# Two PSUM tiles of the item part move to another pool, and the first two inputs to another DMA queue, in a GRU, attention and AUGRU kernel

## The chip, the cores and the metric

The kernel runs on one core of one Trainium2 chip. The metric is device time in microseconds (us). Four runs of the kernel before had a median of 2054.43 us, from 2053.69 to 2054.89.

## What is computed

A recommendation model with 1024 users (B), histories of 100 steps (T) and 128 features. The reference, cut down:

```python
keys = scan(gru_step, h0, x)                       # GRU over T steps
feat = concat([keys, q, keys - q, q * keys])       # q: the item, the same at every step
score = mlp(feat, att_W0..2)                       # 512 -> 80 -> 40 -> 1, relu
attn = softmax(where(mask == 1, score, -inf), over T)
pooled = einsum('bt,btd->bd', attn, keys)
att_seq = pooled.T[:T]
aug = scan(augru_step, h0, (keys, att_seq))        # a second GRU, its update gate weighted by att_seq
attention_feature = aug[sequential_length - 1]
scores = mlp(concat([user, item, hist_sum, item * hist_sum, attention_feature]), ph_W0..2)
```

Since q is the same at all steps, the first attention layer is split: a part of the keys and of q*keys at each step, and an item part, computed once (the kernel's `q0`).

## The kernel before, in words

The batch is split into two halves of 512 columns (HB). Features lie on the 128 partitions. The program has two phases, one after the other.

**GRU phase** (`gru_phase`). A loop over 100 steps s, and in each step over the halves. A step of a half (`Half.gru`) opens gate tiles of 128x512 in PSUM (helper `gate`, L499, matmuls at L501): `ps0` (reset), `ps2` twice (the hidden and the input share of the new state) and `ps1` (update), six matmuls of f32, each of which TensorE runs as two passes. ScalarE takes the sigmoid of the reset gate (L513); VectorE forms `u` (L521) and adds it to the input share (L531); ScalarE takes tanh (L532) and the update gate's sigmoid (L533), both in place; VectorE finishes with `d` (L536, L537) and the new state `hn` (L538). At step 0 there is no old state and only the input matmuls run.

After both halves of step s comes `attend(s - 1)` (L656, matmuls at L663), which writes two tiles `pm`, one a half, with all layers of the attention's MLP for earlier steps packed side by side. Two steps later `take` (L687) reads them: VectorE adds the item part `q0` (L697), ScalarE applies relu (L702). At step 1 alone, `item_part` (L236) runs between the gates and `attend(0)`: for each half a matmul of the item into a tile `pq` (L239), then a ScalarE activation that moves it to `q0` with a bias (L242).

PSUM has eight banks of 128x512 f32. The pool `ps` (tag "g", six buffers) holds the gate tiles, one tile `count`, and at the end of the phase six tiles named `last`; the pool `pa` (tag "a", two buffers) holds `pq`, `pm` and `pt`. A tile that takes a buffer waits until the tile that had it before has been read for the last time. In the compiled program a pool hands its buffers out in the order in which the program's build sees them released: the gate tiles of step 1 lie in banks 0, 3, 4, 5 (half 0: reset, hidden share, input share, update) and 0, 2, 1, 3 (half 1), those of step 2 in 0, 5, 4, 2 and 3, 1, 0, 5; `pq` lies in banks 6 and 7, as do all `pm`.

**Start.** SP's queue issues, in this order: the weights `wih` (L182), `x_first` (L185, step 0 of half 0), the biases `bih` and `bhh` (L124), `x_second` (L189, step 0 of half 1), `whh` (L124), the inputs of steps 1 and 2 (L471), and the attention's weights (L220 to L234). ScalarE's first instruction of the program is an activation on a one-column tile (L198) that brings the table load forward.

**End of the GRU phase.** L876 takes the six `ps` buffers as `last`: two for the softmax (`e`), one for its transposes (`pt`), one for VectorE's pooling products (`kw`), two for the features' matmuls (`f`). In the compiled program they lie in banks 1, 3, 0, 4, 2 and 5. VectorE and GpSimd finish the pooling (L589, L599, L600), VectorE writes it to `s_b` (L937), and eight DMAs store it in `pooled_d` (five on SP's queue, three on ScalarE's, L941 and L1208).

**AUGRU phase** (`augru_phase`). It has one pool for each of banks 0 to 6 and one for bank 7. It loads keys with transposes on TensorE (L1040) that ScalarE copies (L1041), computes first gates (L981), gathers the pooled rows by GpSimd (L144, `att_r`), and opens the first gate tiles (L1054) in banks that are fixed by number in L73: `FREE_BANK, EARLY_BANKS, LATE_BANKS = 6, (2, 5, 6, 0), (3, 4, 1)`; half 1's gates of step 1 in 2, 5, 6, a tile `spare` in 0, half 0's gates in 3, 4, 1. The attention's rows are spread by matmuls at L996 (`first`, `spare`), and then the loop over steps 1 to 99 follows.

Here stand the functions that the change touches:

Of the kernel before, what the change touches and what calls it, by code (L numbers as in the profile page):

```python
# [9 lines left out]
F32 = mybir.dt.float32  # L10
# [9 lines left out]
P = 128  # L20
B = 1024
T = 100
HB = 512
# [55 lines left out]
def kernel(ctx: ExitStack, tc: tile.TileContext, a: dict, out: bass.AP):  # L79
# [26 lines left out]
    nc = tc.nc  # L106
# [73 lines left out]
    def gru_phase(pools):  # L180
# [1 line left out]
        nc.sync.dma_start(out=wih, in_=a["wih"])  # L182
        xp = pools.enter_context(tc.tile_pool(name="xp", bufs=8))
        x_first = xp.tile([P, HB], F32, name="x")
        nc.sync.dma_start(out=x_first, in_=a["hist_x"][0][:, :HB])  # L185
        bih = load("bih", [P, 3])
        bhh = load("bhh", [P, 3])
        x_second = xp.tile([P, HB], F32, name="x")
        nc.sync.dma_start(out=x_second, in_=a["hist_x"][0][:, HB:])  # L189
        whh = load("whh", [P, 3, P])  # L190
        pre = pools.enter_context(tc.tile_pool(name="pre", bufs=1))

# [23 lines left out]
        ps = pools.enter_context(tc.tile_pool(name="ps", bufs=6, space=PSUM))  # L216
        pa = pools.enter_context(tc.tile_pool(name="pa", bufs=2, space=PSUM))
# [17 lines left out]

        def item_part():  # L236
            for i in range(NH):
                pq = pa.tile([P, HB], F32, tag="a", name="pq")
                nc.tensor.matmul(  # L239
                    pq, lhsT=wq[i], rhs=item[:, ts(i, HB)], start=True, stop=True  # L240
                )
                nc.scalar.activation(q0[:, ts(i, HB)], pq, AF.Identity, bias=bm[i])  # L242
# [211 lines left out]
        class Half:  # L454
# [13 lines left out]
            def load(self, t, again=False):  # L468
                if t or again:
                    x = xp.tile([P, HB], F32, name="x")  # L470
                    nc.sync.dma_start(out=x, in_=a["hist_x"][t][:, self.cols])  # L471
                    self.x[t] = x
# [339 lines left out]
        for s in range(T):  # L812
# [36 lines left out]
            if s == 0:  # L849
                attention_weights()  # L850
            else:
                if not staged:
                    next(rest, None)
                if s == 1:
                    item_part()
                attend(s - 1)
# [393 lines left out]
    with ExitStack() as pools, tc.manual_schedule():  # L1250
        gru_phase(pools)
# [79 lines left out]
```

## Time and profile before

| what | value |
|---|---|
| median of 4 runs (lowest to highest) | 2054.43 us (2053.69 to 2054.89) |
| the profiled execution's own time | 2052.77 us |
| span of its profile, first to last instruction | 2050.9 us |
| TensorE (PE) busy | 2022.3 us, 99% of the span |
| VectorE (DVE) busy | 1749.7 us, 85% |
| GpSimd (POOL) busy | 1303.4 us, 64% |
| ScalarE (ACT) busy | 830.6 us, 40% |
| DMA moved | 204.36 MB, mean 100 GB/s |

The page lists, for each engine, busy time and, for groups of instructions, how long the engine was idle just before them and what ended that. A timeline row reads: start in us from the span's start, duration, engine, line, operation, output<-inputs, shape, count of merged instructions, and in brackets the idle time before with its releaser. SPq and ACTq are DMA issues of SP's and ScalarE's queues. PEld is the weight load that precedes each pass of a matmul. Ends of matmuls are modelled and overlap the next one's start, so the distance between starts is the rate. Of the 2050.9 us the GRU phase takes about 1435 to 1447, the AUGRU phase the rest; the two engines that compute most, PE and DVE, are both busy across nearly all of it.

### The profile page before, as it was taken

To read this page: it belongs to the slowest core of one execution; us is meant where nothing else is said; L and a number is where in the kernel's file an instruction comes from. 1 tells how busy PE (TensorE), PEld (TensorE's weight loads), DVE (VectorE), ACT (ScalarE), POOL (GpSimd) and SP (SyncE) were. 2 spreads that over 40 slices of the span, in tenths; PEclk is the share of its full clock that TensorE was granted. 3 is DMA by queue.
4 is the path that set the end of the run, shared out by engine and by line. 5 is a ranking of instruction groups with operands and counts; after the bars stand their busy time and mean duration, and the time that the engine had idled before them with its cause. 6 is when DMAs were issued, how large, how long until landed. Compare 5 with 4: busy or idle time off the path is not lost. (4 is left out here: it accounts for less than half of the span.)

```text
span 2050.9 us, 26797 instructions
## 1 busy us (share of the span) xinstructions
PE 2022.3 (99%) x8320; PEld 978.1 (48%) x8320; DVE 1749.7 (85%) x3050; ACT 830.6 (40%) x1516; POOL 1303.4 (64%) x1299
## 2 busy tenths in 40 slices
PE   8999999999999999999999999999899999999998
PEld 3343343333333333333333333334444556678998
DVE  6888999998989988988889898999567777888886
ACT  3334343343433333433334333434344444445554
POOL 0233939669796959596896868898645434444432
PEclk9999999999999999999999999999999999999999
DMA  4643333223334334333333333332434333333332
GB/s 119 118 94 89 104 99 102 85 83 104 112 101 109 117 97 126 112 97 94 96 115 104 98 95 104 96 98 81 137 104 115 93 90 99 95 96 101 95 77 37
DMA packets 254132, 204.36 MB, mean 100 GB/s; under 512 B 76006, under 2 KB 217034, under 8 KB 253978
## 3 DMA queue, kind: packets, MB, share of 16 engines
q1 hardware_dynamic: 240266, 170.43, 29.4%
q0 software_dynamic: 12128, 31.91, 5.5%
q8 instruction: 68, 1.11, 0.2%
q14 instruction: 86, 0.70, 0.1%
q10 hardware_dynamic: 1584, 0.20, 0.1%
HBM read 146.43 MB, written 54.40 MB: 98 GB/s over the span
## 5 line engine op out<-in xcount | busy, mean ns | idle before, releaser
L501 PE MATMUL ps<-x,wih 128*128 128x512 f32 x1200 | 592.0, 603 | 4.1 <-DMA x<-in_hist_x 4.1
L501 PE MATMUL ps<-hn,whh 128*128 128x512 f32 x1188 | 574.4, 592 | 0.0
L501 PEld LDWEIGHTS ps<-x,wih 128*128 128x128 f32 x1200 | 220.6, 190 | 327.2 <-issue 254.6
L501 PEld LDWEIGHTS ps<-hn,whh 128*128 128x128 f32 x1188 | 225.7, 190 | 284.1 <-issue 274.1
L487 POOL TENSOR_TENSOR xm<-x,m 128x512 f32<-128x512 f32 x200 | 248.3, 1241 | 136.1 <-DMA m<-mask_d 135.6
L532 ACT ACTIVATE ps<-ps,bih 128x512 f32<-128x512 f32 x200 | 132.4, 662 | 478.7 <-DVE ps L531 478.7
L513 ACT ACTIVATE r<-ps,brz 128x512 f32<-128x512 f32 x200 | 137.5, 688 | 382.0 <-PE ps L501 381.1
L488 POOL TENSOR_TENSOR hist<-hist,xm 128x512 f32<-128x512 f32 x200 | 267.7, 1338 | 15.7
L600 POOL TENSOR_TENSOR pooled<-pooled,kw 128x512 f32<-128x512 f32 x191 | 254.0, 1330 | 15.0
L599 POOL TENSOR_TENSOR kw<-kt,e 128x512 f32<-128x512 f32 x191 | 219.5, 1149 | 64.7 <-DVE e L772 64.6
L168 POOL DMA_INDIRECT rows<-keys_d,idx_k x204 | 198.8, 975 | 81.6 <-POOL rows L167 75.5
L576 DVE TENSOR_TENSOR kq<-hn,item 128x512 f32<-128x512 f32 x200 | 224.5, 1162 | 0.0
L663 PE MATMUL pm<-hn,wk 128*32 128x512 f32 x1200 | 211.6, 596 | 3.8 <-ACT q L242 2.3
L663 PE MATMUL pm<-kq,wkq 128*32 128x512 f32 x1200 | 209.2, 592 | 0.0
L1066 ACT ACTIVATE c<-ph,bh 128x96 f32<-128x96 f32 (+41 forms) x198 | 96.5, 488 | 256.7 <-PE ph L1058 256.6
L663 PE MATMUL pm<-mv,w 128*32 128x512 f32 (+1 forms) x808 | 195.8, 598 | 1.3 <-DVE e L753 1.3
L697 DVE TENSOR_TENSOR f<-pm,q 128x512 f32<-128x512 f32 x200 | 128.3, 683 | 52.6 <-PE pm L663 52.6
L536 DVE TENSOR_TENSOR d<-hn,ps 128x512 f32<-128x512 f32 x198 | 136.0, 687 | 34.9 <-ACT ps L532 32.5
L167 POOL COPY rows<-rest 128x1 f32<-128x1 f32 x204 | 38.7, 190 | 199.0 <-DVE rest L1095 197.7
L1082 DVE TENSOR_TENSOR pu<-pu,c 128x96 f32<-128x96 f32 (+41 forms) x197 | 88.4, 449 | 88.5 <-ACT c L1066 84.6
L537 DVE TENSOR_TENSOR d<-ps,d 128x512 f32<-128x512 f32 x200 | 138.4, 692 | 23.6 <-ACT ps L533 6.5
L531 DVE TENSOR_TENSOR ps<-ps,u 128x512 f32<-128x512 f32 x200 | 140.0, 700 | 21.6 <-PE ps L501 0.5
(180 smaller groups left out, 3018.2 us busy)
## 6 DMA issues: line engine op xcount, KB each, us to landing
x<-in_hist_x SPq DMA_DIRECT2D x212, 256.0 KB
keys_d<-kt SPq DMA_DIRECT2D x46, 1024.0 KB
m<-mask_d SPq DMA_DIRECT2D x200, 128.0 KB
keys_d<-kt SPq DMA_DIRECT2D x64, 64.0 KB
rows<-keys_d,idx_k POOLq DMA_INDIRECT x204, 2.9
s_b<-mv SPq DMA_DIRECT2D x200, 8.0 KB
at<-att_d SPq DMA_DIRECT2D x34, 48.0 KB
mask_i<-in_mask SPq DMA_DIRECT2D x8, 200.0 KB
```

Source lines behind the costliest of these rows:

```text
L168: nc.gpsimd.indirect_dma_start(out=r[:, k, :], out_offset=None, in_=keys_d[q], in_offset=bass.IndirectOffsetOnAxis(ap=idx_k[:, k, i : i + ...
L487: nc.gpsimd.tensor_mul(d, x, m)
L488: nc.gpsimd.tensor_add(acc, acc, d)
L501: nc.tensor.matmul(p, lhsT=w[:, g, :], rhs=v, start=(j == 0), stop=(j == len(parts) - 1),)
L513: nc.scalar.activation(r, pr, AF.Sigmoid, bias=brz[:, 0:1])
L531: nc.vector.tensor_add(pi, pi, u)
L536: nc.vector.tensor_sub(d, h, pi)
L537: nc.vector.tensor_mul(d, pz, d)
L576: nc.vector.tensor_mul(kq, h, item[:, self.cols])
L599: eng.tensor_mul(d, k, w)
L600: eng.tensor_add(acc, acc, d)
L663: nc.tensor.matmul(p[i][s, :], lhsT=w[:, s], rhs=v, start=start, stop=stop)
```

## The change

The two first inputs are loaded through ScalarE's DMA queue instead of SP's, ahead of everything else on ScalarE. The two `pq` tiles come from the pool `ps` (tag "g") instead of `pa` (tag "a"). The whole diff:

```diff
@@ -182,11 +182,11 @@
         nc.sync.dma_start(out=wih, in_=a["wih"])
         xp = pools.enter_context(tc.tile_pool(name="xp", bufs=8))
         x_first = xp.tile([P, HB], F32, name="x")
-        nc.sync.dma_start(out=x_first, in_=a["hist_x"][0][:, :HB])
+        nc.scalar.dma_start(out=x_first, in_=a["hist_x"][0][:, :HB])
         bih = load("bih", [P, 3])
         bhh = load("bhh", [P, 3])
         x_second = xp.tile([P, HB], F32, name="x")
-        nc.sync.dma_start(out=x_second, in_=a["hist_x"][0][:, HB:])
+        nc.scalar.dma_start(out=x_second, in_=a["hist_x"][0][:, HB:])
         whh = load("whh", [P, 3, P])
         pre = pools.enter_context(tc.tile_pool(name="pre", bufs=1))
 
@@ -235,7 +235,7 @@
 
         def item_part():
             for i in range(NH):
-                pq = pa.tile([P, HB], F32, tag="a", name="pq")
+                pq = ps.tile([P, HB], F32, tag="g", name="pq")
                 nc.tensor.matmul(
                     pq, lhsT=wq[i], rhs=item[:, ts(i, HB)], start=True, stop=True
                 )
```

`FREE_BANK`, `EARLY_BANKS` and `LATE_BANKS` (L73) stay as they are.

## The prediction

> **What bounds the kernel now.** I read the page's first part (who is busy), then whom TensorE (PE) waits for, then the timeline of the stretches that the change touches.
>
> ```profile
> PE 2022.3 (99%) x8320; PEld 978.1 (48%) x8320; DVE 1749.7 (85%) x3050; ACT 830.6 (40%) x1516; POOL 1303.4 (64%) x1299
> ```
>
> PE works 99% of the span, so only time in which it stands or runs slowly can be won. The view of PE's waits from 0 to 1400 us is short (us in total, times, longest):
>
> ```profile
> PE ps L501 <- DMA x<-in_hist_x: 4.1, 1, 4.1
> PE pm L663 <- ACT q L242: 2.3, 1, 2.3
> PE pm L663 <- DVE e L753: 1.3, 1, 1.3
> ```
>
> The change touches the first (the first input) and the second (the item part). After the second PE runs at its own rate: step 2 starts at 30.06 and step 5 at 72.27 in the timeline, (72.27 - 30.06)/3 = 14.07 a step, and the step from 1384.89 to 1398.96 still takes 14.07. So what PE wins before 30 us should last to the end of the GRU phase. The timeline from there (rows of several engines):
>
> ```profile
> 20.79 0.69 ACT L513 ACTIVATE r<-ps,brz 128x512 f32<-128x512 f32 x1
> ...
> 21.12 0.69 DVE L537 TENSOR_TENSOR d<-ps,d 128x512 f32<-128x512 f32 x1
> ...
> 21.75 1.88 PE L239 MATMUL pq<-item,wq 128*128 128x512 f32 x4
> ...
> 21.84 0.69 DVE L538 TENSOR_TENSOR hn<-ps,d 128x512 f32<-128x512 f32 x1
> ...
> 24.62 0.65 ACT L533 ACTIVATE ps<-ps,brz 128x512 f32<-128x512 f32 x1
> ...
> 25.19 1.27 ACT L242 ACTIVATE q<-pq,bm 128x512 f32<-128x512 f32 x2
> ...
> 25.93 0.62 PE L663 MATMUL pm<-hn,wk 128*32 128x512 f32 x2 [2.30 <-ACT q L242]
> ...
> 26.51 0.11 PEld L663 LDWEIGHTS pm<-hist,w 128*32 128x32 f32 x1 [0.36 <-ACT q L242]
> ...
> 30.06 1.13 PE L501 MATMUL ps<-x,wih 128*128 128x512 f32 x2
> ```
>
> PE has the item part done by about 23.5, but `attend(0)` writes its `pm` into the two banks that `pq` fills, and ScalarE empties them only at 25.19, behind half 1's tanh and sigmoid of step 1. The second `pm` waits once more, in the middle of `attend(0)`.
>
> The start, in the timeline and in the DMA view of 0 to 6 us (GB/s in slices of 0.15 us):
>
> ```profile
> 0.74 1.28 ACT L198 ACT_TABLE_LOAD   x1 [0.74 <-PEq L1318]
> ...
> 0.75 0.39 SPq L182 DMA_DIRECT2D wih<-in_wih  x1
> 1.19 0.42 SPq L185 DMA_DIRECT2D x<-in_hist_x  x1
> ```
>
> ```profile
> GB/s 0 0 0 0 0 0 0 0 0 0 0 61 184 276 317 311 263 280 328 287 274 262 170 59 47 206 259 300 232 253 222 246 287 369 294 331 277 263 232 273
> ```
>
> The issues come 0.44 apart, and the DMA engines move some 260 to 330 GB/s from 1.95 on, with a hollow at 3.45 to 3.75. By the packet records, `wih` runs from 1.76 to 2.75 and `x_first` from 2.35 to 3.63. PE starts at 4.06, 0.43 after the last byte.
>
> **The item part.** Nothing is added: the same two matmuls and two activations, in other banks. Three steps.
>
> 1. Does `pq` still start at 21.75? It takes the two banks of `ps` that were released first. In the compiled order step 2 takes 0 and then 5 at this place: half 1's reset gate, read by ScalarE from 20.79 to 21.48, and half 0's update gate, read at L537 until 21.81. The first is free before 21.75, the second before 22.61, when `pq` of half 1 is due (two passes of 0.43 later). No wait. If the pool went by turn instead, `pq` would get half 0's input share, read until 22.53 (L538), and start 0.85 later. I take 0, with 0.85 as the other end.
> 2. The wait goes. Four passes at 0.43 end at 21.75 + 1.72 = 23.47. At step 4 `attend` follows its gates by 0.10 (67.74 + 0.86 = 68.60, against its start at 68.70), so `attend(0)` starts at 23.57, not 25.93: 2.36 less. What is next late? Its inputs: the state `hn` of step 0 (15.69), `kq` (16.85 + 1.28 = 18.13), the weights `w12`, whose last issue is at 18.43 now and earlier after, and which no row shows PE waiting for. None is later than 23.57.
> 3. The second wait goes. `attend(0)` takes 30.06 - 25.93 = 4.13, but 72.27 - 68.70 = 3.57 at step 4: in the timeline the streams that should run four abreast are out of step after 26.51. Another 0.56.
>
> Step 2 would then start at 23.57 + 3.57 = 27.14, that is 2.92 earlier. It needs half 0's `hn` (22.53) and a free bank: six have been released by 26.94 (half 1's L538). VectorE is done at 26.94 and then waited 3.30 us for `pm`, so its next row (L697) follows PE. `q0` is ready at 26.46 for it: the activations keep their place on ScalarE. The gain is 2.92, between 2.92 - 0.85 = 2.07 and 2.92 as far as these rows go.
>
> **The first inputs.** ScalarE issues two DMAs before its table load. I cost these two issues on ScalarE at nothing: 2 x 0.44 move the load from 0.74 to 1.63 and its end to 2.91, and ScalarE's next work is at 6.14; if that cover were gone it would be 0.9. On SP the rest moves up by 0.9, of which nothing is waited for. `x_first` is issued at 0.74 instead of 1.19, so 0.45 is the most it can win. But it then shares the engines with `wih`: 192 + 256 KB = 458,752 bytes at 280 GB/s are 1.64, from 1.75 to 3.39, plus 0.43, so PE starts near 3.8: 0.25 to 0.3. At the low end, ScalarE's table load stays ahead of the issues: `x_first` goes out at 2.07, 0.88 later than now, and PE loses 0.88. I take a gain of 0.3, since the first table load belongs to L198, behind the DMAs in the program; ends -0.88 and +0.45. [...]
>
> **Banks behind the GRU phase.** The names in L73 now point at other tiles of the phase's end. That costs something only if a first gate falls on a bank that is read late. The last read of any is VectorE's L600, which ends at 1446.88, and PE's wait view shows `pr` at L1054 waiting for just that (0.3 us) before the change too. Behind it are these rows:
>
> ```profile
> 1450.39 1.12 PE L1054 MATMUL pu<-k,wu 128*128 128x510 f32 x2 [1.49 <-ACT k L1041]
> ...
> 1459.63 1.22 PE L996 MATMUL first<-ident,att_r 128*128 128x128 f32 x4 [2.17 <-DMA att_r<-pooled_d,idx]
> ```
>
> PE is idle for 2.17 before the gathered rows arrive, and these come from VectorE by a DMA and GpSimd, not from a PSUM bank. That cover hides up to 2.17; I take 0.
>
> **The sum.** 2.92 + 0.3 = 3.2 us. The profiled execution's 2052.77 (span 2050.9 and 1.9 around it) would be 2049.6; the median of the runs is 1.7 above that execution, and I put the gain on it: 2054.43 - 3.2 = **2051.2 us**, 0.16% less. That is below the 0.2% (4.1 us, so 2050.3 and 2058.5) that a measurement of this kernel can tell from no change.
>
> **Rivals.**
>
> *More.* The starts of PE's weight loads are 0.86 apart up to 8.45 and 0.43 after, and from 1459 to 1463 the granted clock is 0.57: a drop behind the idle stretch. If the drop stays away when the program lies 3 us earlier, the four passes of `first` (1.22 there, 0.92 at 1456.55) and the eight of `spare` (1.91, later 1.05) are 1.2 shorter, about half of it on the path through L1007: 0.5 to 1.2 more, 2050.0 to 2050.7. For: the phases move against each other. Against: 2.17 of idle time stays. [...]
>
> *Less.* The table load comes first: 2.92 - 0.88 = 2.0 gained, 2052.4.
>
> *Nothing.* The end of the GRU phase follows VectorE, not PE (PE waits 1.54 for L697 at 1414.63), and VectorE, if it were late all along, would not move: 2054.4. Against: in the loop VectorE waits 50 times for `pm`.
>
> *Slower.* The pool gives `pq` a bank that half 1 still uses. The place is 21.75: with half 1's input share, read until 26.94 (L538), `pq` starts at 27.0, `attend(0)` runs from 28.82 to 32.39, 2.3 after 30.06; less 0.3, that is 2056.4, and 2057.6 with the late table load. It decides from a release at 30.06 - 3.57 - 0.10 - 1.72 - 0.06 = 24.6 on; only half 1's update gate (26.21) and input share are later. Against: the order of step 2 puts these two last.
>
> **How the numbers follow.** As forecast 0.58 (2051.2, by itself 2050.4 to 2052.0), more 0.14, less 0.13, nothing 0.08, slower 0.07. The range of 2050.0 to 2053.4 leaves out the last two and the far end of "more". Faster by over 0.2% is most of "more" and a little of the forecast's edge: 0.13. Slower by over 0.2% needs the slower rival and one more loss: 0.03. The rest, 0.84, is within 0.2%.
>
> **What would show it.** In the new profile: no PE wait on `q`; `pq` at about 21.5 and `attend(0)` directly behind it, 3.6 long; step 2 at 26.8; steps of 14.07; PE's first matmul at 3.8; and PE's waits at L1054 and L996 as they are. I am wrong if `pq` itself waits, if the first matmul starts after 4.06, if L1054 waits past 1457, or if the early gain is gone by 1415.

## The result and the profile after

The changed kernel takes 2052.64 us (median of 32 runs, 2050.62 to 2056.38), the kernel before 2054.92 us in the runs beside it (52 runs, 2052.83 to 2057.79): 2.28 us less, a ratio of 0.999 with a 95% interval from 0.9985 to 0.9995, that is 1.0 to 3.1 us. The forecast was 3.2 us less, 2051.2 us with a range of 2050.0 to 2053.4, and "within 0.2%"; the kernel before measured 2054.92 here where the forecast had started from 2054.43. The profiled execution took 2051.42 us, its span 2049.6. The view of PE's waits from 0 to 1400 us, after:

```profile
PE ps L501 <- DMA x<-in_hist_x: 4.4, 1, 4.4
PE pm L663 <- DVE e L753: 1.3, 1, 1.3
```

The wait on `q` (2.3 before) is gone. The wait on the first input did not shrink: 4.4 instead of 4.1. The timeline of the start, rows of SP, ACT, PE and DVE (start, duration, engine, line, what, idle before):

```profile
0.75 0.39 SPq L182 DMA_DIRECT2D wih<-in_wih  x1
...
0.75 0.41 ACTq L185 DMA_DIRECT2D x<-in_hist_x  x1
1.19 0.45 ACTq L189 DMA_DIRECT2D x<-in_hist_x  x1
1.67 1.28 ACT L198 ACT_TABLE_LOAD   x1 [1.67 <-PEq L1318]
...
4.39 8.02 PE L501 MATMUL ps<-x,wih 128*128 128x512 f32 x14 [4.39 <-DMA x<-in_hist_x]
...
21.09 0.69 ACT L513 ACTIVATE r<-ps,brz 128x512 f32<-128x512 f32 x1
...
21.88 1.96 PE L239 MATMUL pq<-item,wq 128*128 128x512 f32 x4
23.76 0.62 PE L663 MATMUL pm<-hn,wk 128*32 128x512 f32 x2
...
25.49 1.27 ACT L242 ACTIVATE q<-pq,bm 128x512 f32<-128x512 f32 x2
...
26.55 0.69 DVE L538 TENSOR_TENSOR hn<-ps,d 128x512 f32<-128x512 f32 x1
27.33 1.13 PE L501 MATMUL ps<-x,wih 128*128 128x512 f32 x2
27.54 1.29 DVE L697 TENSOR_TENSOR f<-pm,q 128x512 f32<-128x512 f32 x2 [0.30 <-PE pm L663]
```

`x_first` leaves at 0.75 and the table load follows behind it, as forecast, and still PE starts later in this profile (in a second one, e11 below, at 4.10). `attend(0)` follows `pq` directly and takes 27.33 - 23.76 = 3.57, exactly a steady step's, although `q` is emptied only at 25.49. Step 2 starts 2.73 earlier than in the profile of before. VectorE ends at 27.24 and waits 0.30, instead of 3.30, for `pm`: by these rows VectorE binds if PE comes more than another 0.3 earlier (an estimate from that wait).

The end of the GRU phase, timeline of PE after:

```profile
1447.87 1.12 PE L1054 MATMUL pu<-k,wu 128*128 128x510 f32 x2 [0.62 <-ACT k L1041]
...
1457.36 1.22 PE L996 MATMUL first<-ident,att_r 128*128 128x128 f32 x4 [2.32 <-DMA att_r<-pooled_d,idx]
1458.38 1.91 PE L996 MATMUL spare<-ident,att_r 128*128 128x128 f32 x8
1460.17 2.02 PE L1058 MATMUL pr<-h,wr 128*128 128x510 f32 x2
```

PE still waits 2.32 for the gathered rows, so the banks of L73 cost nothing. Of the 2.73, 2.27 are left here (1457.36 against 1459.63). Then `pr` takes 2.02 instead of 1.14; in the profile of before its row is

```profile
1462.44 1.14 PE L1058 MATMUL pr<-h,wr 128*128 128x510 f32 x2
```

By the trace's clock records PE ran at half rate (a granted 0.50) from 1455.2 for two stretches of 3.41 us, and for one more from 1438.1, where before it was one in all, from 1459.1 (the last 8 to 12 us of the program, at half rate in every profile, are not counted here or below). The span ends 1.3 earlier. These two profiles alone would thus put the gain at 1.3, the medians at 2.3.

### The profile page after: what moved, and what is told of

Its sections match the earlier page's. It is cut to its first block, busy times and chain, and to the rows that moved or that the text cites. A ratio compares the mean times of both kernels' runs of the same rounds, so it can differ in the third digit from the quotient of the medians.

```text
span 2049.6 us, 26798 instructions
## 1 busy us (share of the span) xinstructions
PE 2023.9 (99%) x8320; PEld 977.9 (48%) x8320; DVE 1749.3 (85%) x3050; ACT 830.5 (41%) x1516; POOL 1304.3 (64%) x1299
## 5 line engine op out<-in xcount | busy, mean ns | idle before, releaser
L501 PE MATMUL ps<-x,wih 128*128 128x512 f32 x1200 | 591.6, 602 | 4.4 <-DMA x<-in_hist_x 4.4
L501 PE MATMUL ps<-hn,whh 128*128 128x512 f32 x1188 | 574.4, 592 | 0.0
L501 PEld LDWEIGHTS ps<-x,wih 128*128 128x128 f32 x1200 | 220.5, 190 | 327.3 <-issue 254.1
L501 PEld LDWEIGHTS ps<-hn,whh 128*128 128x128 f32 x1188 | 225.7, 190 | 284.1 <-issue 274.8
L532 ACT ACTIVATE ps<-ps,bih 128x512 f32<-128x512 f32 x200 | 132.4, 662 | 480.5 <-DVE ps L531 480.5
```

Source lines behind the costliest of these rows:

```text
L501: nc.tensor.matmul(p, lhsT=w[:, g, :], rhs=v, start=(j == 0), stop=(j == len(parts) - 1),)
```

## The experiments

Theory A: the gain is the wait for ScalarE's two item activations, and the inputs bring nothing. Rival B: the inputs bring 0.3, as forecast. The first two runs do one part of the change alone.

**e1: the item part alone** (the `pq` line of the diff).

> Only the item part moves to the gates' pool; both first inputs stay on SP's queue. Theory A (the whole gain is the two waits on the item part's banks, and the new queue gives nothing back): first matmul at 4.06 us as before, no PE wait on q, step 2 starts near 27.1 us (30.06 - 2.92), and the time is 2.5 to 2.9 us under the kernel before, so at least as good as the whole change (2.3 us under it). Rival B (the first inputs carry a part, as the prediction's term of 0.3 us had it): 0.3 us or more worse than the whole change, 2.0 us under the kernel before or less.

2052.02 us against 2054.35, ratio 0.9987 (0.9978 to 0.9996): 2.33 less, the whole change's gain. PE's timeline of e1:

```profile
22.66 1.88 PE L239 MATMUL pq<-item,wq 128*128 128x512 f32 x4
...
28.04 1.13 PE L501 MATMUL ps<-x,wih 128*128 128x512 f32 x2
```

First matmul 4.37 with the very instructions that started at 4.06 before; from the first matmul of `pq` to step 2 it takes 28.04 - 22.66 = 5.38 (before: 8.31), 2.93 less. But step 2 itself is only 2.02 earlier than before, since `pq` came at 22.66 instead of 21.75. Against A that is a miss of 0.9 in the place, not in the wait.

**e2: the inputs alone** (the two `nc.scalar.dma_start` lines).

> Only the two first inputs move to ScalarE's queue; the item part stays where it was. Theory A: first matmul near 4.39 us as in the whole change (0.33 later than before), the wait on q as before (2.3 us), step 2 starts 0 to 0.35 us later than 30.06 apart from where the clock opens, time within 0.4 us of the kernel before. Rival B (the prediction's term): first matmul near 3.8 us, time 0.3 us under the kernel before.

2054.81 us against 2054.35, ratio 1.0002 (0.9993 to 1.0011): no change. First matmul 4.35, wait on `q` 2.67, step 2 at 30.20. B's first matmul at 3.8 us is refuted; the times alone, with an interval of 1.4 less to 2.3 more, could not tell 0.3 from nothing.

**e3 and e4: one input each on ScalarE's queue**, with the item part of e1. The edit of e3, against e1; e4 makes the same one for `x_first`.

```diff
-        nc.sync.dma_start(out=x_second, in_=a["hist_x"][0][:, HB:])
+        nc.scalar.dma_start(out=x_second, in_=a["hist_x"][0][:, HB:])
```

> Item part moved; of the inputs only x_second goes by ScalarE's queue, x_first stays on SP's behind wih. Theory C (two queues that start at the same time feed each other's packets more slowly, whoever needs them): wih, alone on SP's queue from 1.76 to 2.75 us before, takes until 3 us or later, and the first matmul starts at 4.2 us or later although what it needs comes by SP. Rival D (ScalarE's queue is itself slow to start): wih and x_first keep their times and the first matmul starts at 4.06 us.

> Item part moved; only x_first goes by ScalarE's queue, x_second stays on SP's in its place before. Theory C: wih and x_first still overlap, wih ends near 3.5 us and the first matmul starts between 4.0 and 4.3 us, a little earlier than the 4.39 of the whole change because x_second no longer competes. Rival D: as the whole change, 4.39 us, since x_first alone decides.

First matmul at 4.89 (e3) and 4.16 (e4), in one profile each (2054.53 and 2053.46 us). In e3 what PE needs comes by SP alone, and yet it is late: by the packet records `wih` ends at 3.50, against 2.75 before and 2.70 in e1; in e4 at 3.54, in the whole change at 3.69. Over all profiles it ends at 3.46 to 3.69 in the five with two queues and at 2.65 to 2.86 in the eight with SP alone, so this is no jitter. That is C, as far as it says that the two queues share. The DMA view of 0 to 6 us (GB/s in slices of 0.15 us), of e1, of e5 below (SP alone as well) and of the changed kernel:

```profile
GB/s 0 0 0 0 0 0 0 0 0 0 0 51 154 236 307 352 321 328 300 273 329 209 111 61 116 206 193 218 259 297 270 290 301 410 290 256 191 236 205 232
```

```profile
GB/s 0 0 0 0 0 0 0 0 0 0 0 20 72 113 154 307 416 403 359 341 410 301 138 36 103 154 191 273 311 297 290 259 335 379 318 287 266 263 300 191
```

```profile
GB/s 0 0 0 0 0 0 0 0 0 0 0 51 41 72 126 184 283 287 297 393 413 328 222 397 313 399 356 360 416 325 316 250 294 294 239 290 386 365 386 417
```

The slow first slices of the changed kernel (41 to 184 up to 2.4) are not what the second queue does: e5, with SP alone, has 72 to 154 up to 2.25, while e1 has 154 to 307 there. Over 1.75 to 3.60 us as a whole the view gives 246 to 250 GB/s in the eight profiles with SP alone and 251 to 273 in the five with two queues. A second queue hardly added to the rate, it shared it. `wih` came later, and `x_first` was not in earlier: its last packet comes at 3.62 to 3.78 in the four profiles that load it by ScalarE's queue, at 3.50 to 3.82 in the eight with SP alone. In e3 `wih` lost to a tile that nobody needs yet. That the first matmul of one and the same start (SP alone) lies anywhere from 4.04 to 4.37 in five profiles is jitter of the size of the disputed term; part of it lies between the last packet of the two tiles and the matmul, 0.38 to 0.70 us in ten profiles (those without the zero matmuls of e7 below).

**e5: one tile in each pool**, half 0's `pq` in the attention's pool.

```diff
-                pq = ps.tile([P, HB], F32, tag="g", name="pq")
+                pq = (pa, ps)[i].tile([P, HB], F32, tag="ag"[i], name="pq")
```

> As the item part alone, but only half 1's item tile lies in the gates' pool; half 0's stays in the attention's pool. Theory A (PE takes its work in order, so whichever attention tile still waits for ScalarE holds all that is behind it): attend(0) starts directly behind the item part, as without a wait, but stops inside at the tile that still shares a bank until ScalarE's item activation of that half has ended; from the first item matmul to step 2 some 6 to 7 us, between 8.31 (before) and 5.38 (item part alone). Rival B (the first wait is the whole gain): 5.4 to 5.9 us.

One profile (2052.58 us). From `pq` to step 2: 29.53 - 22.04 = 7.49, over A's 6 to 7 and far from B's 5.9. PE's timeline of e5:

```profile
23.85 0.62 PE L663 MATMUL pm<-hn,wk 128*32 128x512 f32 x2
...
24.32 0.59 PE L663 MATMUL pm<-hist,w 128*32 128x512 f32 x1
26.00 0.59 PE L663 MATMUL pm<-hist,w 128*32 128x512 f32 x1 [1.09 <-issue]
...
29.53 1.12 PE L501 MATMUL ps<-x,wih 128*128 128x512 f32 x2
```

`attend(0)` starts at once, stops until 26.00, and then runs with its streams out of step: 5.68 in all. The view names no releaser for the stop (`issue`); ScalarE starts on `q` at 25.21 there, as it starts at 25.19 before, where PE is released at 25.93. Half the banks gave 0.8 of the 2.9.

**e6: the banks as before, the item part earlier.** In the loop over the halves, after half 0 of step 1:

```diff
+                if half.i == 0:
+                    if s == 1:
+                        item_part()
...
-                if s == 1:
-                    item_part()
```

> The kernel before with its banks and its queue, but the item part is issued between the gates of half 0 and half 1 of step 1, 3.4 us earlier on PE and ahead of half 1's tanh on ScalarE. Theory A (what costs is the wait for ScalarE, not the pool): no PE wait on q, attend(0) in 3.57 us, step 2 some 2.9 us earlier against the first matmul than before, time 2 to 3 us under the kernel before, the same as with the banks of the gates' pool. Rival B (half 1's chain is delayed by the two activations of 1.27 us ahead of it, and with it step 2): 1 to 2 us under the kernel before.

2051.65 us against 2054.10, ratio 0.9988 (0.9979 to 0.9997): 2.45 less, the same as by other banks. PE's timeline:

```profile
23.42 0.62 PE L663 MATMUL pm<-hn,wk 128*32 128x512 f32 x2
...
27.00 1.12 PE L501 MATMUL ps<-x,wih 128*128 128x512 f32 x2
```

`pq` is at 16.43, `attend(0)` has no wait, and step 2 comes 22.96 after the first matmul (before: 26.00). So it is the wait that costs, and the pool was one way to lose it.

What remained was why `pq` came at 22.66 in e1, and why 2.9 at the wait are 2.3 at the end. **Theories E and G**: (E) PE's first work runs at half rate until the granted clock (the share of full speed that the profile records for PE) rises, and the moment differs from run to run; (G) before, the wait on `q` swallowed that, and now it is on the path. e8 and e11 are the two kernels unchanged (one profile each, 2056.38 and 2052.71 us), e7 and e9 put zero matmuls in front, with and without the item part:

```diff
+        cold = const.tile([P, P], F32, name="cold")
+        nc.vector.memset(cold, 0.0)
...
+        warm = pa.tile([P, HB], F32, tag="a", name="warm")
+        for _ in range(7):
+            nc.tensor.matmul(warm[:, :P], lhsT=cold, rhs=cold, start=True, stop=True)
```

> The kernel before, unchanged, profiled a second time. Theory E: the first matmul may move by 0.3 us or so and the clock's rise by up to 2 us against the first profile, and the clock's drop near 1459 us may last one or two stretches of 3.41 us, with the same program. Rival: first matmul 4.06, rise at 8.43 and one drop at 1459.1 again.

> The whole change, unchanged, profiled a second time. Theory G: the first matmul between 4.1 and 4.5 us; step 2 starts at 27.3 us if the clock rises near 8 us and up to 1 us later if it rises near 10 us, whereas in the two profiles of before step 2 came at 30.06 and 30.27 with rises at 8.4 and 10.3 us. Rival: step 2 at 27.3 whenever the clock rises.

> Item part alone, and in front of everything seven matmuls of 128x128 zeros on PE while it waits for the first input (about 3 us at the slow rate; their result is not read). Theory E (PE's first microseconds of work run at half rate until the granted clock rises, at a moment that differs from run to run): the rise comes before or soon after the first real matmul, so the slow stretch behind it shrinks from 3.3 to 5.9 us to 0 to 3, step 2 starts at about 26 us instead of 28, and the time is a further 1 to 2 us down, 3.5 to 4.5 us under the kernel before. Rival F (a rise needs real work, or the start is bound by something else): no change against the item part alone, 2.3 us under the kernel before.

> The kernel before (item part in the attention's banks, inputs on SP) with the same seven zero matmuls in front. Theory G (in the kernel before the wait on q is a cushion: step 2 starts when VectorE's and ScalarE's chain from the first matmul is through, so that what PE gains or loses by the clock's rise vanishes in the wait): pq starts near 21 us, the wait on q grows by as much, step 2 starts 0 to 0.8 us earlier against the first matmul than in the two profiles of before (26.0 and 26.1 us behind it), and the time falls by 0 to 0.9 us. Rival H (the clock's rise is worth the same with or without the wait): 1.8 us under the kernel before, as it brought on top of the item part.

The table reads the first matmul on real data, the clock's rise (clock records; in the timeline the weight loads' starts go from 0.86 to 0.43 apart there) and PE's starts:

| profile | first | rise | pq | attend(0) | step 2 | step 2 - first |
|---|---|---|---|---|---|---|
| before | 4.06 | 8.43 | 21.75 | 25.93 | 30.06 | 26.00 |
| e8, before again | 4.17 | 10.26 | 22.71 | 26.14 | 30.27 | 26.10 |
| e2, inputs alone | 4.35 | 7.65 | 21.53 | 26.07 | 30.20 | 25.85 |
| e9, before with warm start | 4.21 | 4.75 | 20.17 | 24.94 | 30.61 | 26.39 |
| after | 4.39 | 7.94 | 21.88 | 23.76 | 27.33 | 22.95 |
| e11, after again | 4.10 | 9.59 | 22.37 | 24.18 | 27.75 | 23.65 |
| e1, item part alone | 4.37 | 9.95 | 22.66 | 24.47 | 28.04 | 23.67 |
| e7, e1 with warm start | 4.21 | 7.11 | 21.30 | 23.18 | 26.76 | 22.54 |

With the wait (first three), `pq` lies from 17.18 to 18.54 after the first matmul, but `attend(0)` only from 21.72 to 21.97 and step 2 from 25.85 to 26.10: in e8 VectorE works almost without a pause from 9.5 us on (its timeline to 27 us lists two waits behind that, 0.21 and 0.73), and ScalarE's `q` follows it (at 25.40, behind L532, which waited 2.56 for VectorE, and L533). Without the wait (after, e11, e1, and e3 and e4 with 22.98 and 23.83), step 2 comes 22.95 to 23.83 after, later by 0.3 to 0.4 us for each us that the rise lies later behind the first matmul. The moment of the rise is not free: in all thirteen profiles the time from the rise to every fall and from there to the next rise is a whole multiple of 3.4133 us (1450.66 is 425 of them, 20.48 is 6). Rise and falls thus lie on a grid, and the grid's place against the program's start differs from run to run.

In e8 `pq` lies 0.85 later behind the first matmul than before, and the wait itself is 0.75 shorter:

```profile
22.71 1.88 PE L239 MATMUL pq<-item,wq 128*128 128x512 f32 x4
26.14 0.62 PE L663 MATMUL pm<-hn,wk 128*32 128x512 f32 x2 [1.55 <-ACT q L242]
```

e7 takes 2050.01 us against 2054.10, ratio 0.9979 (0.997 to 0.9988): 4.1 less, by the medians 1.8 more than e1 brought, though the intervals of the two (2.5 to 6.2 and 0.8 to 4.5) overlap. e9, the same matmuls with the wait in place, takes 2054.36 against 2054.38, ratio 1.0001 (0.9992 to 1.001): nothing, which refutes H's 1.8. PE's timeline of e9, and its granted clock (PEclk, third number from the end) from 20 to 25 and 25 to 29 us:

```profile
20.17 1.88 PE L244 MATMUL pq<-item,wq 128*128 128x512 f32 x4
24.94 0.82 PE L668 MATMUL pm<-hn,wk 128*32 128x512 f32 x2 [2.89 <-ACT q L247]
```

```profile
20.00:25.00 5.00, 2.11 (x7) 0.64 (x7) 4.53 (x8) 2.44 (x5) 0.00 (x0) 1.00 0.69 155
25.00:29.00 4.00, 4.00 (x23) 1.81 (x27) 0.91 (x2) 0.46 (x1) 0.00 (x0) 0.57 0.75 167
```

`pq` is 1.6 earlier than before, but only 0.6 of that goes into the wait, and `attend(0)` starts 1.0 earlier. Then the clock falls at 25.2, behind the idle time, and `attend(0)` takes 5.67 instead of 4.13. Step 2 comes 26.39 after the first matmul, later than G expected; with 4.13 it would have come 24.86 after it (an estimate: 24.94 + 4.13 - 4.21), earlier than G's 25.2 to 26.1. So the wait and the fall of the clock behind it together took what the warm start had won, the fall the larger part (an estimate: 5.67 - 4.13 = 1.54 against the 0.6). That the cushion alone takes all of it, as G has it, is not shown, nor whether the clock fell in the other ten runs of e9.

**e10: the drop at the end of the GRU phase**, e7 and before the first weight rows:

```diff
-        first_state(0, pa.tile([P, HB], F32, tag="a", name="first"))
+        first = pa.tile([P, HB], F32, tag="a", name="first")
+        for _ in range(2):
+            nc.tensor.matmul(first, lhsT=ident, rhs=gates[0][0], start=True, stop=True)
+        first_state(0, first)
```

> The item part with the warm start, and in the AUGRU phase two more matmuls of 128x512 into the tile first, while PE waits for the gathered rows (1.7 us of the 2.2 to 2.4 us it is idle; the next matmuls overwrite the tile). Theory E: the granted clock no longer drops between 1455 and 1465 us, or for one stretch of 3.41 us less, and the time is 0.3 to 1.2 us under the item part with the warm start alone, near 4.5 to 5 us under the kernel before. Rival: the drop stays, since it was earned in the idle time before, or the two matmuls reach into the critical start of first: 0 or 0.5 us slower.

2048.91 us against 2054.38, ratio 0.9974 (0.9963 to 0.9984): 5.5 less, by the medians 1.4 less than e7 (E: 0.3 to 1.2), the best version here, and the runs lie within 2048.14 to 2049.63, a spread of 1.5 us where e7 had 4.9. PE's timeline and the granted clock of 1452 to 1459 and 1459 to 1463:

```profile
1453.70 1.98 PE L1224 MATMUL first<-first_u,ident 128*128 128x512 f32 x4 [0.66 <-ACT k L1046]
1455.52 0.83 PE L1001 MATMUL first<-ident,att_r 128*128 128x128 f32 x6
1456.69 0.49 PE L1001 MATMUL first<-ident,att_r 128*128 128x128 f32 x2 [0.34 <-DMA att_r<-pooled_d,idx]
```

```profile
1452.00:1459.00 7.00, 4.93 (x25) 3.35 (x26) 1.39 (x2) 1.48 (x3) 5.42 (x6) 1.00 0.19 56
1459.00:1463.00 4.00, 4.00 (x18) 2.18 (x17) 1.99 (x3) 1.32 (x2) 0.95 (x1) 1.00 0.15 43
```

Here the clock stays up, by the clock records from 5.47 to 2039.8. The stretch from the start of the last gate matmul of the GRU phase (L501) to a fixed matmul of the AUGRU phase (L1054, at 1513.65 in before) is 104.05 in e10, 104.72 with one slow stretch of 3.41 us (before), 105.30 to 106.48 with two (e5, e2, e3) and 105.71 to 107.60 with three (after, e1, e4, e6, e9, e11, e8, e7); from there to the end of the span it is 537.0 to 537.4 in every profile. So the slow stretches, which differ between runs of one kernel (one in the first profile of before, three in e8), go with 0.7 to 3.6 us, and their place counts as well as their number. Not all of this is the two matmuls' doing: e10 also lacks a fall that nine other profiles have between 1413 and 1442, ahead of them, and that before, e2 and e3 lack too. All of it is read off single profiles, and the intervals of e10 and e7 (3.3 to 7.6 and 2.5 to 6.2 us less) overlap.

## Why the prediction was right or wrong

- **The wait on `q` goes, and `attend(0)` takes 3.57**: right. e1 shows 2.93 less from `pq` to step 2, against 2.92 worked out.
- **`pq` starts without a wait on its new banks**: right to 0.2. `pq` started at 21.88, behind ScalarE's `r` (21.09 + 0.69 = 21.78), 0.19 after PE was free (20.83 + 0.86). The margin of 0.27 that I read off one profile goes when the clock rises early: in e10, with a rise at 5.47, `pq` came 0.42 after PE was free. A late bank, the slower rival, did not occur; it was not tried by itself.
- **The inputs bring 0.3**: wrong as far as can be told; e2 shows no gain, and the first matmul came at 4.39 and 4.10 (e11), not at 3.8. A first matmul after 4.06 was named as a sign of being wrong. The failed step was the transfer at 280 GB/s from 1.75 on. Before the change the same 458,752 bytes took from 1.76 to 3.63 by the packet records, 245 GB/s with the slow first slices, and `x_first` began (2.35) while `wih` was still under way (to 2.75): by these records the transfer did not stand waiting for its issue. With two queues the same bytes took from 1.76 to 3.69 (e11: 3.62). The issue did move to 0.75, and the table load did stay behind it, so the rival "less" did not occur. Of the 0.44 that the issue came earlier little came through: by the packet records the first packet of the inputs came at 2.24 instead of 2.35, and the last one of `x_first` at 3.62 to 3.78 (four profiles) where SP alone gave 3.50 to 3.82 (eight).
- **What PE wins before 30 us it keeps**: mostly. In the profiles 2.73 became 2.54 at 1412.09 (against 1414.63) and 2.27 at 1457.36. Not every step of the loop takes 14.07, however. The one near 270 us took 14.62 in before and 15.40 in e8, with the same kernel; the one near 1354 us, in which PE waits for VectorE's `e`, took 15.52 to 17.41 over all profiles. From step 2 to step 99 it is 1368.30 to 1370.03 in the four profiles with the wait on `q` and 1369.25 to 1371.06 in eight without it, on average 0.9 more: some of the gain may be lost there, as the rival "nothing" had it for all of it, but the spread is as large. And taking PE's start of `pq` from one profile was the second step that failed: 21.75 held for a rise at 8.43, and over ten profiles without the warm start the rise lies from 7.65 to 10.26, which after the change is on the path. From the first matmul, step 2 gained 25.98 - 23.34 = 2.64 (means of three profiles before, and of after, e11, e1, e3, e4 and e6), not 2.92.
- **Banks behind the GRU phase cost nothing**: right; the wait at L996 is 2.32.
- **The rival "more"**, that the drop near 1459 stays away: it did not; the profile of after has three slow stretches, as has the second one of before. Its size, 0.5 to 1.2 for the one stretch, fits the 0.67 between before and e10 (104.72 and 104.05). The stretches last 3.41 or 6.83 us (6.83 from 1455.2 in after), and their number differs between profiles of one kernel (one in before, three in e8).
- **Sum**: 2.6 and nothing for the inputs, against 3.2; the medians say 2.28, with an interval of 1.0 to 3.1. The time lay within the range although one term was wrong: the item part made up nearly all of the sum, and the range was wider than the disputed term. Whether the 0.3 between 2.6 and 2.28 is lost in the loop or is the spread of the runs stays open.

## What to carry to other kernels

A wait that two tiles in one bank cause can be undone by another bank (2.33 us less in e1) or by issuing the work earlier (2.45 us less in e6), and what that wins ends where the next engine binds (here VectorE, 0.3 us further, an estimate from its idle time in after). A wait on the path is also a cushion: it takes up what jitters ahead of it (0.75 of 0.85 us in e8), and when it goes the jitter becomes visible (step 2 comes 22.95 to 23.83 after the first matmul in the six profiles after, e11, e1, e3, e4 and e6, 25.85 to 26.10 in the three with it). Warming the clock paid only in the kernel without the wait (by the medians 1.8 us more in e7 than in e1, with overlapping intervals; nothing in e9), though in e9, by the estimate above, a fall of the clock had a larger part in that than the cushion (1.54 against 0.6 us). Compare profiles of one and the same kernel before a term of a few tenths is believed (first matmul at 4.06 and 4.17, rise at 8.43 and 10.26 in the two of before).

## What the runs showed of the hardware that was not expected

- Two DMA queues that start together moved 251 to 273 GB/s from 1.75 to 3.60 us where one moved 246 to 250, and the weights that everyone waits for landed 0.6 to 1.0 us later (last packet of `wih` at 3.46 to 3.69 in five profiles instead of 2.65 to 2.86 in eight).
- The granted clock changed only at whole multiples of 3.4133 us from its first rise, in all thirteen profiles (in before 425 of them, 1450.66 us, to the first fall). The length of an idle time alone did not tell whether it would fall: 2.89 us of idle time on PE were followed by half rate in e9 (at 25.2), 2.67 were not in e2; PE's 3.00 us of waiting for `k` (L981) were followed by it in after (at 1438.1) and not in before.
- The clock rose without data of the kernel on PE: behind matmuls of zeros from 1.06 us on it rose at 4.75 to 7.11 (e7, e9, e10) instead of 7.65 to 10.26 (the ten profiles without them).
